# Attention layer of a graph network: column-tiled denominators, products on GpSimd, normalisation on ScalarE, next batch's rows made early

## The chip, the cores and the metric

One core of a Trainium2 chip. The metric is the time of one launch on the device in microseconds; smaller is better. An execution is called fast when it lies within 1.5% of the fastest of its kernel, and all runs quoted here are fast ones. Engines in the profile: PE is TensorE's matmuls, PEld its weight loads, DVE VectorE, ACT ScalarE, POOL GpSimd, SP SyncE, which issues most of the DMA transfers.

## The reference, cut to what matters

Eight batches of 2048 nodes with 256 features go through two layers. Layer 0, the only one that the change touches, is masked attention with four heads of 64:

```
h = relu(layernorm(x))                           # the "hidden rows"
q, k, v = h @ Wq.T + bq, ...                     # 4 heads x 64
s = clip(q k^T / 8, -10, 10);  s = -10 where adj == 0
ctx = softmax(s) @ v                             # per head
out = layernorm(ctx @ Wo.T + bo + h) * gamma + beta
x = x + out
```

Layer 1 is another graph attention over the same adjacency.

## The kernel before

A group is 512 query rows of a batch; a batch has four groups. Per group the kernel walks over the keys in eight steps of 256. A step has, for each pair of heads, two score matmuls with their mask step on VectorE and their exponential on ScalarE, and the weighted sum of the values. The sums of the exponentials (the denominators of the softmax) are gathered for half a group, 16 step-and-pair tiles in two halves of 8, then inverted and multiplied on, half a group late:

```python
def add_keys(b, g, j, p):                        # GpSimd halves TensorE's work
    t = work.tile([P, 2, 512], F32, tag="es", name="es", bufs=2)
    nc.gpsimd.tensor_tensor(t, es[b, g, j, p, 0], es[b, g, j, p, 1], op=ALU.add)

def denominators(b, g, j, p):
    # ...  two 64-column tiles at once, one row of pz per step and pair
    for s in range(2):
        nc.tensor.matmul(pz[0][ds(s * D, D), :], strip[:, 63 - r : 127 - r], t[:, s, :], ...)
    if last:                                     # once per half group
        nc.scalar.copy(zs, pz[0])                # sums to DRAM, back spread over 128 partitions
        # ... zd <- zs, zi <- zd
        nc.vector.reciprocal(zi, zi)
        # ... zr <- zi

def scale(b, g, j, p):                           # one tile of 128 x 512
    rz = work.tile([P, 512], F32, tag="rz", name="rz", bufs=4)
    for s in range(2):                           # each of two rows to 64 partitions
        nc.sync.dma_start(rz[ds(s * D, D), :], src[s : s + 1, :].to_broadcast([D, 512]))
    # ... the product:
    nc.vector.tensor_tensor(t, t, rz, op=ALU.mult)
    nc.gpsimd.tensor_tensor(dst, dst, t, op=ALU.add)      # the accumulation

def finish(b, g):
    # ... output projection po from acc; hidden row, bias and residual on VectorE into y
    layernorm_stats(work, y, ymv, yrs)           # ends with the power (var + eps)^-0.5 on GpSimd
    for i in range(4):
        normalize(y[:, i, :], y[:, i, :], ymv[:, i, 0:1], yrs[:, i : i + 1])   # VectorE
    nc.gpsimd.tensor_tensor(y, y, rg, op=ALU.mult)
    # ... + beta, + x, then a store to x1d from GpSimd's queue
```

The whole program is recorded first. A scheduler then lays down the order of each engine's queue, and each engine works through its own in that order, waiting where an operand or buffer isn't ready.

The softmax here doesn't subtract the row's maximum and nothing guards it: scores larger than these inputs give would overflow.

Of the kernel before, what the change touches and what calls it, by code (L numbers as in the profile page):

```python
# [25 lines left out]
def kernel(  # L26
# [74 lines left out]
    with ExitStack() as c0:  # L101
# [10 lines left out]
        R = NP * CHALF  # L112
        zd = dram.tile([B, NG, 2, 2, R, 512], F32, tag="zd", name="zd")
        zr = dram.tile([B, NG, 2, 2, R, 512], F32, tag="zr", name="zr")

# [16 lines left out]
        strip = wp.tile([P, 127], F32, tag="strip", name="strip")  # L132
        nc.vector.memset(strip, 0.0)
        nc.vector.memset(strip[:, 63:64], 1.0)
# [8 lines left out]
        for j2 in range(NB // 2):  # L143
            tag = ("hT", "kT")[j2 % 2]
            a_sb = big.tile([P, 2, N], I32, tag=tag, name=f"a_sb_{j2}")
            nc.sync.dma_start(a_sb, adj_t[ts(j2, 2 * P), :].rearrange("(j p) i -> p j i", p=P))
            for k in range(2):
                j = 2 * j2 + k
                e01 = work.tile([P, N], BF16, tag="e", name=f"e01_{j}", bufs=5)
                nc.vector.tensor_scalar(e01, a_sb[:, k, :], 0.0, None, op0=ALU.not_equal)  # L150
                nc.scalar.activation(m0t[:, j, :], e01, AF.Copy, bias=-LIM, scale=2.0 * LIM)
                g01 = work.tile([P, N], BF16, tag="e", name=f"g01_{j}", bufs=5)
                nc.vector.tensor_scalar(g01, a_sb[:, k, :], 0.0, None, op0=ALU.is_gt)
                m1b = work.tile([P, N], I8, tag="ut", name=f"m1b_{j}", bufs=18)
                nc.scalar.copy(m1b, g01)
                nc.gpsimd.dma_start(m1d[:, j, :], m1b)
                for i in range(NIG):
                    for c in range(2):
                        nc.tensor.matmul(
                            degs[i][:, c, :], ones_b, g01[:, ts(2 * i + c, 512)],  # L160
                            start=(j == 0), stop=(j == NB - 1),
                        )
        nn = work.tile([P, N], BF16, tag="es", name="nn", bufs=2)
# [31 lines left out]
        hT, kT, v, mv, rs = {}, {}, {}, {}, {}  # L195

        def prepare0(b):
            hT[b] = big.tile([P, FC, N], F32, tag="hT", name=f"hT_{b}")
            kT[b] = big.tile([P, FC, N], F32, tag="kT", name=f"kT_{b}")
            v[b] = big.tile([P, NB, H, D], F32, tag="v", name=f"v_{b}")  # L200
            mv[b] = work.tile([P, NB, 2], F32, tag="mv", name=f"mv_{b}")
            rs[b] = work.tile([P, NB], F32, tag="rs", name=f"rs_{b}")
            for g in range(NG):
                xg = load_x(b, g, "x")
                layernorm_stats(work, xg, mv[b][:, ts(g, 4), :], rs[b][:, ts(g, 4)])
                pts = ps_sc.tile([P, FC, 512], F32, tag="sc", name="pts")
                for i in range(4):
                    ib = 4 * g + i
                    z = work.tile([P, F], F32, tag="z", name="z", bufs=3)
                    normalize(z, xg[:, i, :], mv[b][:, ib, 0:1], rs[b][:, ib : ib + 1])  # L210
                    for c in range(FC):
                        nc.tensor.transpose(pts[:, c, ts(i, P)], z[:, ts(c, P)], ident)
                for c in range(FC):
                    nc.scalar.activation(hT[b][:, c, ts(g, 512)], pts[:, c, :], AF.Relu)
                hg = hT[b][:, :, ts(g, 512)]
                project_t("k", hg, kT[b][:, :, ts(g, 512)])
                pv = ps_sc.tile([P, 4, F], F32, tag="sc", name="pv")
                for i in range(4):
                    for c in range(FC):
                        nc.tensor.matmul(  # L220
                            pv[:, i, :], hg[:, c, ts(i, P)], wts["v"][:, c, :],
                            start=(c == 0), stop=(c == FC - 1),
                        )
                for i in range(4):
                    nc.vector.tensor_tensor(
                        v[b][:, 4 * g + i, :, :].rearrange("p h d -> p (h d)"),
                        pv[:, i, :], reps["v"], op=ALU.add,
                    )

            project_q(b, 0)  # L230
# [7 lines left out]
        def scores(b, g, j, p, k):  # L238
# [7 lines left out]
            e = work.tile([P, 2, 512], F32, tag="e", name="e", bufs=5)  # L246
# [3 lines left out]
            es[b, g, j, p, k] = e  # L250

        sums, pu, ut, pz = {}, {}, {}, {}

        def add_keys(b, g, j, p):

            t = work.tile([P, 2, 512], F32, tag="es", name="es", bufs=2)
            nc.gpsimd.tensor_tensor(t, es[b, g, j, p, 0], es[b, g, j, p, 1], op=ALU.add)  # L257
            sums[b, g, j, p] = t

        def weighted(b, g, j, p, k):  # L260
            if k == 0:
                pu[0] = ps_u.tile([P, 512], F32, tag="u", name="pu")
            e = es.pop((b, g, j, p, k))
            for s in range(2):
                nc.tensor.matmul(  # L265
                    pu[0][ds(s * D, D), :], v[b][:, 2 * j + k, 2 * p + s, :], e[:, s, :],
                    start=(k == 0), stop=(k == 1),
                )
            if k == 1:
                t = work.tile([P, 512], F32, tag="ut", name="ut", bufs=18)  # L270
                nc.scalar.copy(t, pu[0])  # L271
                ut[b, g, j, p] = t

        def denominators(b, g, j, p):

            r = p * CHALF + j % CHALF
            if j % CHALF == 0 and p == 0:
                pz[0] = ps_z.tile([P, 512], F32, tag="z", name="pz")
            t = sums.pop((b, g, j, p))
            last = j % CHALF == CHALF - 1 and p == NP - 1  # L280
            for s in range(2):
                nc.tensor.matmul(  # L282
                    pz[0][ds(s * D, D), :], strip[:, 63 - r : 127 - r], t[:, s, :],
                    start=(j % CHALF == 0 and p == 0), stop=last,
                )
            if last:
# [3 lines left out]
                for s in range(2):  # L290
                    nc.sync.dma_start(zd[b, g, w, s], zs[ds(s * D, R), :])
                n = 2 * R * 512 // P
                zi = work.tile([P, n], F32, tag="zi", name="zi", bufs=2)
                flat = "s r i -> (s r i)"
# [5 lines left out]
        def scale(b, g, j, p):  # L300

            src = zr[b, g, j // CHALF, :, p * CHALF + j % CHALF, :]
            rz = work.tile([P, 512], F32, tag="rz", name="rz", bufs=4)
            for s in range(2):
                nc.sync.dma_start(rz[ds(s * D, D), :], src[s : s + 1, :].to_broadcast([D, 512]))
# [4 lines left out]
            if j == 0:  # L310
                nc.vector.tensor_tensor(dst, t, rz, op=ALU.mult)
            else:
                nc.vector.tensor_tensor(t, t, rz, op=ALU.mult)  # L313
                nc.gpsimd.tensor_tensor(dst, dst, t, op=ALU.add)  # L314

        def finish(b, g):
            xg = load_x(b, g, "xr")
            y = work.tile([P, 4, F], F32, tag="y", name="y", bufs=1)
            for i in range(4):
                ib = 4 * g + i  # L320
                po = ps_m.tile([P, F], F32, tag="m", name="po")
                for p in range(NP):
                    nc.tensor.matmul(  # L323
                        po, acc[b, g][:, p, ts(i, P)], wts["o"][:, p, :],
                        start=(p == 0), stop=(p == NP - 1),
                    )
                z = work.tile([P, F], F32, tag="z", name="zr", bufs=3)
                normalize(z, xg[:, i, :], mv[b][:, ib, 0:1], rs[b][:, ib : ib + 1])
                nc.vector.tensor_tensor(y[:, i, :], po, reps["o"], op=ALU.add)
                nc.vector.scalar_tensor_tensor(  # L330
                    y[:, i, :], z, 0.0, y[:, i, :], op0=ALU.max, op1=ALU.add
                )
            ymv = work.tile([P, 4, 2], F32, tag="ymv", name="ymv")
            yrs = work.tile([P, 4], F32, tag="yrs", name="yrs")
            layernorm_stats(work, y, ymv, yrs)
            for i in range(4):
                normalize(y[:, i, :], y[:, i, :], ymv[:, i, 0:1], yrs[:, i : i + 1])
            rg = reps["g"].unsqueeze(1).to_broadcast([P, 4, F])
            re = reps["e"].unsqueeze(1).to_broadcast([P, 4, F])
            nc.gpsimd.tensor_tensor(y, y, rg, op=ALU.mult)  # L340
            nc.gpsimd.tensor_tensor(y, y, re, op=ALU.add)
# [3 lines left out]

        later = {}

        order = [prepare0, scores, add_keys, weighted, denominators, scale, project_q, finish]
# [3 lines left out]

        n = 0
        for b in range(B):
            at(n, prepare0, b)
            for g in range(NG):
                if g + 1 < NG:
                    at(n + 24, project_q, b, g + 1)
                for j in range(NJ):
                    for p in range(NP):  # L360
                        for k in range(2):
                            at(n, scores, b, g, j, p, k)
                            at(n + 2, weighted, b, g, j, p, k)
                            n += 1
                        at(n - 1, add_keys, b, g, j, p)
                        at(n + 4, denominators, b, g, j, p)
                    if j % CHALF == CHALF - 1:
                        for i in range(R):
                            at(n + 11 + i, scale, b, g, j - CHALF + 1 + i // NP, i % NP)
                at(n + 24, finish, b, g)  # L370
# [248 lines left out]
```

## Time and profile before

| | before |
|---|---|
| time | 5824.49 us, median of 3 runs (5818.94 to 5836.31) |
| end of the last output projection of layer 0 | 3690 us |
| TensorE's waiting in layer 0 (below) | 454 us |
| granted TensorE clock | 0.963 of full speed |

"TensorE's waiting" is my own count from the trace: for every two matmuls that follow each other, the distance of their starts less the usual distance of such a pair (0.43 to 0.53 us), summed where it is over 0.1 us. It includes matmuls that run slow for a while after a stop.

First, what the reciprocals' tiles (rz) do. This is the tile's view: operation, engine, count, then least, median and largest duration in ns; below, what ended the idle time ahead of the operations on this tile.

```profile
L305 SPq DMA_DIRECT2D rz<-zr x1024: 444/594/1547, 177.5 to 3672.7; - x171
...
  DMA rz<-zr: 89.6, 90
```

1024 loads (two a tile), and in the whole run engines stood idle 89.6 us for them. The second view lists waits by pairs: engine and line that waited, what it waited for, total in us, times, longest.

```profile
PE sc L242 <- DVE e L248: 181.2, 96, 6.0
...
DVE e L248 <- POOL es L257: 103.4, 36, 3.6
...
DVE y L93 <- POOL yrs L90: 51.1, 32, 2.7
```

TensorE's chief wait is for the mask step, because VectorE frees the scores' PSUM buffers; VectorE's wait for the power (yrs) is 1.6 us a group.

### The profile page before, as it was taken

The page shows a single profiled execution, that of the slowest core. Times are in us where ns is not written, and L with a number is a line of the kernel's source. Part 1 is how long each engine was busy: PE and PEld are TensorE (multiplying, and loading weights), DVE is VectorE, ACT ScalarE, POOL GpSimd, SP SyncE. Part 2 cuts the span into 40 slices and gives each one's busy share as a digit, 9 for nine tenths or more (in the row PEclk, how much of TensorE's full clock was granted, in tenths as well). Part 3 has the DMA queues.
Part 4 walks back from the last instruction along what each step waited for, and adds up shares of the span by engine and source line. Part 5 has one row for each costly group of instructions (what it writes and reads, how often), then busy time and mean ns, then how long its engine had stood idle before and what let it go on. Part 6 is the DMA issues. An engine that isn't in the chain of part 4 may idle for free.

```text
span 5821.8 us, 50880 instructions
## 1 busy us (share of the span) xinstructions
PE 5352.1 (92%) x17648; PEld 1757.2 (30%) x17648; DVE 4122.9 (71%) x5366; ACT 1750.8 (30%) x2441; POOL 2648.0 (45%) x1599
## 2 busy tenths in 40 slices
PE   6998998998998998998998999499999999999999
PEld 2223223223223222322322322233333333333333
DVE  4675676676676666567566667588888888888887
ACT  5443443443443443443343344100010010000100
POOL 2665665665665666566566566412120312212121
PEclk8999999999999999999999999799999999999999
DMA  5121111112121111111111121201010110101010
GB/s 184 46 60 52 53 52 61 43 55 68 38 57 58 51 53 52 48 56 58 49 53 58 40 60 53 104 8 51 8 58 0 58 37 22 51 8 58 0 44 15
DMA packets 173651, 288.63 MB, mean 50 GB/s; under 512 B 40240, under 2 KB 91312, under 8 KB 167088
## 3 DMA queue, kind: packets, MB, share of 16 engines
q1 hardware_dynamic: 162640, 247.36, 13.8%
q0 software_dynamic: 10752, 38.02, 1.8%
q8 instruction: 138, 2.26, 0.2%
q14 instruction: 121, 0.99, 0.1%
HBM read 243.08 MB, written 42.21 MB: 49 GB/s over the span
## 4 chain that ended last, share of the span: by engine, by line
PE 65%; DVE 11%; issue 8%; DMA 7%; POOL 7%; SPq 1%; ACT 1%; DVEq 0%; POOLq 0%; ACTq 0%
PE av L503 21%; PE sc L242 15%; PE pu L265 13%; PE pz L282 5%; PE pp L181 3%; DVE w L491 3%; DVE e L248 3%; POOL nnm L477 3%; PE po L323 2%; DMA rz<-zr 2%; PE pv L220 2%; DVE ut L313 2%; PE pq L451 1%; POOL acc L314 1%; DMA x<-x1d 1%
## 5 line engine op out<-in xcount | busy, mean ns | idle before, releaser
L248 DVE SCALAR_TENSOR_TENSOR e<-sc,m0t 128x1024 f32<-128x1024 f32 x1024 | 1243.2, 1220 | 819.2 <-PE sc L242 714.7
L503 PE MATMUL av<-w,q 128*65 128x512 f32 x4096 | 1795.3, 595 | 28.6 <-DVE w L491 28.6
L257 POOL TENSOR_TENSOR es<-e 128x1024 f32<-128x1024 f32 x512 | 1225.5, 2397 | 896.7 <-PE pz L282 804.6
L491 DVE SCALAR_TENSOR_TENSOR w<-rrep,tcol,m1t 128x1024 f32<-128x1024 f32 x1024 | 1352.1, 1346 | 236.3 <-PE av L503 232.2
L242 PE MATMUL sc<-qT,kT 64*128 64x512 f32 x4096 | 1242.9, 655 | 182.7 <-DVE e L248 181.2
L249 ACT ACTIVATE e<-e 128x1024 f32<-128x1024 f32 x1024 | 1083.8, 1058 | 1038.0 <-DVE e L248 1007.5
L265 PE MATMUL pu<-e,v 128*64 128x512 f32 x4096 | 1196.6, 639 | 0.5
L503 PEld LDWEIGHTS av<-w,q 128*65 128x65 f32 x4096 | 559.9, 139 | 1150.7 <-issue 1061.4
L314 POOL TENSOR_TENSOR acc<-acc,ut 128x512 f32<-128x512 f32 x448 | 651.2, 1466 | 378.9 <-DVE ut L313 376.8
L539 POOL TENSOR_TENSOR x<-x,hp 128x256 f32<-128x256 f32 x128 | 148.0, 1170 | 1469.5 <-DVE hp L535 1469.1
L242 PEld LDWEIGHTS sc<-qT,kT 64*128 64x128 f32 x4096 | 330.8, 188 | 1046.8 <-DVE e L248 599.9
L282 PE MATMUL pz<-es,strip 128*64 128x512 f32 x2048 | 564.2, 607 | 3.1 <-POOL es L257 3.1
L313 DVE TENSOR_TENSOR ut<-ut,rz 128x512 f32<-128x512 f32 x448 | 523.8, 1186 | 52.5 <-DMA rz<-zr 51.7
L271 ACT COPY ut<-pu 128x512 f32<-128x512 f32 x512 | 298.2, 582 | 687.8 <-PE pu L265 686.8
L265 PEld LDWEIGHTS pu<-e,v 128*64 128x64 f32 x4096 | 215.0, 137 | 797.6 <-ACT e L249 387.5
L510 ACT COPY u<-av 65x1024 f32<-65x1024 f32 x64 | 64.5, 1008 | 1242.5 <-PE av L503 1242.5
L282 PEld LDWEIGHTS pz<-es,strip 128*64 128x64 f32 x2048 | 153.4, 140 | 307.4 <-issue 282.5
L477 POOL TENSOR_SCALAR nnm<-mean,nnc 128x256 f32<-128x256 f32 x128 | 197.1, 1557 | 7.4 <-ACT mean L474 7.3
L323 PE MATMUL po<-wo,acc 128*128 128x256 f32 x512 | 153.2, 421 | 50.6 <-POOL acc L314 39.3
L93 DVE TENSOR_SCALAR z<-x,mv,rs 128x256 f32<-128x256 f32 x256 | 119.0, 509 | 93.1 <-POOL rs L90 50.7
L89 POOL TENSOR_SCALAR bnve<-mv 128x4 f32<-128x4 f32 x64 | 27.9, 436 | 268.4 <-DVE mv L87 268.4
L86 DVE BATCH_NORM_STATS2 bnst<-x 128x6 f32<-128x256 f32 x256 | 97.8, 405 | 72.0 <-DMA x<-x1d 47.0
(82 smaller groups left out, 2959.8 us busy)
## 6 DMA issues: line engine op xcount, KB each, us to landing
rz<-zr SPq DMA_DIRECT2D x1024, 128.0 KB
rrep<-rd SPq DMA_DIRECT2D x32, 1024.0 KB
a_sb<-in_adj_t_dram SPq DMA_DIRECT2D x8, 2048.0 KB
x<-in_x_dram SPq DMA_DIRECT2D x32, 512.0 KB
xr<-in_x_dram SPq DMA_DIRECT2D x32, 512.0 KB
x1d<-y POOLq DMA_DIRECT2D x32, 512.0 KB, 5.2
x<-x1d SPq DMA_DIRECT2D x32, 512.0 KB
out_dram<-x POOLq DMA_DIRECT2D x32, 512.0 KB, 3.5
```

The costliest lines, as they stand in the source:

```text
L242: nc.tensor.matmul(sc[:, s, :], kT[b][hs, p, ts(2 * j + k, P)], qT[b, g][hs, p, :], start=True, stop=True,)
L248: nc.vector.scalar_tensor_tensor(e, sc, -LIM, m, op0=ALU.max, op1=ALU.min)
L249: nc.scalar.activation(e, e, AF.Exp, scale=SCALE)
L257: nc.gpsimd.tensor_tensor(t, es[b, g, j, p, 0], es[b, g, j, p, 1], op=ALU.add)
L265: nc.tensor.matmul(pu[0][ds(s * D, D), :], v[b][:, 2 * j + k, 2 * p + s, :], e[:, s, :], start=(k == 0), stop=(k == 1),)
L271: nc.scalar.copy(t, pu[0])
L282: nc.tensor.matmul(pz[0][ds(s * D, D), :], strip[:, 63 - r : 127 - r], t[:, s, :], start=(j % CHALF == 0 and p == 0), stop=last,)
L313: nc.vector.tensor_tensor(t, t, rz, op=ALU.mult)
L314: nc.gpsimd.tensor_tensor(dst, dst, t, op=ALU.add)
L477: nc.gpsimd.tensor_scalar(nnm[b][:, i, :], mean, nnc[:, i : i + 1], None, op0=ALU.mult)
L491: nc.vector.scalar_tensor_tensor(w, rrep[b, h][:, ts(ig, 1024)], tcol[b][:, j, h : h + 1], m1t[:, j, ts(ig, 1024)], op0=ALU.max, op1=ALU.mult,
L503: nc.tensor.matmul(pav[0][:, k, :], q1[b][:, j, h, :], w[:, ts(k, 512)], start=(j == 0), stop=(j == NB - 1),)
```

## The change

The intent: take 512 sums off GpSimd by giving the exponentials straight to TensorE in four 32-column tiles; give GpSimd the products instead, so that VectorE is free for the mask steps; normalise on ScalarE; make the next batch's hidden rows during the batch before.

```diff
-        def denominators(b, g, j, p):
+        def denominators(b, g, j, k):
...
-            for s in range(2):
+            for h in range(H):
                 nc.tensor.matmul(
-                    pz[0][ds(s * D, D), :], strip[:, 63 - r : 127 - r], t[:, s, :],
+                    pz[0][ds(32 * h, 32), :], strip[:, 31 - r : 63 - r],
+                    es[b, g, j, k, h // 2][:, h % 2, :],
+                    start=first, stop=last, tile_position=(0, 32 * h),
                 )
...
             rz = work.tile([P, 512], F32, tag="rz", name="rz", bufs=4)
-            for s in range(2):
-                nc.sync.dma_start(rz[ds(s * D, D), :], src[s : s + 1, :].to_broadcast([D, 512]))
+            nc.sync.dma_start(
+                rz,
+                bass.AP(
+                    tensor=src.tensor, offset=src.offset,
+                    ap=[[CHALF * 512, 2], [0, D], [1, 512]],
+                ),
+            )
...
-                nc.vector.tensor_tensor(t, t, rz, op=ALU.mult)
+                nc.gpsimd.tensor_tensor(t, t, rz, op=ALU.mult)
                 nc.gpsimd.tensor_tensor(dst, dst, t, op=ALU.add)
...
         def finish(b, g):
             y = work.tile([P, 4, F], F32, tag="y", name="y", bufs=1)
             for i in range(4):
-                ... hidden row, bias and residual on VectorE after the projection
+                nc.scalar.activation(
+                    y[:, i, :], xg[:, i, :], AF.Relu,
+                    bias=nb[b][:, ib : ib + 1], scale=rs[b][:, ib : ib + 1],
+                )
...
             for i in range(4):
-                normalize(y[:, i, :], y[:, i, :], ymv[:, i, 0:1], yrs[:, i : i + 1])
+                nc.scalar.activation(y[:, i, :], y[:, i, :], AF.Identity, bias=..., scale=...)
...
-            at(n, prepare0, b)
+            for g in range(NG):
+                at(n - S + 4 + 7 * g if b else -1, hidden, b, g)
+                at(n + 8 * g - (2 if g else 0), project_k, b, g)
+                at(n + 8 * g, project_v, b, g)
...
-                at(n + 24, finish, b, g)
+                at(n + 22, finish, b, g)
```

The cuts leave out that e has six buffers for five, that the products are recorded two steps earlier (n + 9 for n + 11), and that the bias bo is added on GpSimd.

## The prediction

> **What bounds the kernel now.** I read the page from the top, then the groups, then the chain of waits inside one batch of layer 0 (1600 to 1700 us), then the timeline of the same stretch. Layer 0 runs to about 3690 us, layer 1 after it is not touched.
>
> ```profile
> PE 5352.1 (92%) x17648; PEld 1757.2 (30%) x17648; DVE 4122.9 (71%) x5366; ACT 1750.8 (30%) x2441; POOL 2648.0 (45%) x1599
> PE   6998998998998998998998999499999999999999
> ```
>
> TensorE is the bound in both layers; the recurring 8 in layer 0 says that it also waits. In the steady stretch it does not: one pair of heads and 256 keys is two scores, two weighted sums and one denominator, 1.06 + 1.01 + 1.06 + 1.01 + 0.86 = 4.99 us without a gap.
>
> ```profile
> 1604.27 1.06 PE sc L242 x4
> 1605.32 1.01 PE pu L265 x4
> 1606.33 1.06 PE sc L242 x4
> 1607.39 1.01 PE pu L265 x4
> 1608.40 0.86 PE pz L282 x4
> ```
>
> A batch has 64 of these. The starts of the query projections in the timeline are about 66, 98.4, 99 and 184 us apart, 446 us for a batch, while 64 x 4.99 is 319. Projections, transposes and the output product add some 70, matmuls of a pair that the scheduler split (they run alone, at twice the price) some 10. I counted the excess of each gap between matmul starts over its usual value: about 47 us a batch, 375 in all, is waiting. It comes in two places per group of 512 rows.
>
> ```profile
> 1623.15 1.01 PE pu L265 x4
> ...
> 1625.46 2.12 issue
> 1627.58 1.72 POOL acc L314
> ...
> 1629.62 1.05 POOL yrs L90
> ...
> 1633.02 1.14 DVE e L248
> ...
> 1634.21 1.37 PE sc L242 x4
> 1635.58 1.90 PE pu L265 x4
> ```
>
> First, in the finish of the group before: the little power on GpSimd (yrs) stands behind sums and accumulations in that queue; VectorE waits for it ahead of the next mask step, and TensorE runs dry for 4 us, then goes slow for a few matmuls (1.90 for 1.01). Second, 50 us later, the products with the reciprocals crowd VectorE: another 5 us.
>
> ```profile
> 1672.08 3.25 DMA rz<-zr
> ...
> 1680.53 1.22 DVE e L248
> ...
> 1681.79 2.08 PE sc L242 x4
> ```
>
> So a group loses about 11 us, and the start of each batch some 18 more. The two operations that change places, with mean time and what they waited for:
>
> ```profile
> L314 POOL TENSOR_TENSOR acc<-acc,ut 128x512 f32<-128x512 f32 x448 | 651.2, 1466 | 378.9 <-DVE ut L313 376.8
> L313 DVE TENSOR_TENSOR ut<-ut,rz 128x512 f32<-128x512 f32 x448 | 523.8, 1186 | 52.5 <-DMA rz<-zr 51.7
> ```
>
> **What the Trainium skill says.** TensorEngine Tiling (Array Packing), Available Configurations and Key Properties: 128x32 gives four independent tiles, and changing the tiling mode drains TensorE. The trace agrees on the drain: last pass of a weighted sum to a score takes 0.53 us, to a denominator of the same 64-column mode 0.43. TensorE: Matmul & The Clock Gate, Part 1 on queue depths: VectorE and ScalarE are strict FIFO, which is what the 1629 to 1634 wait shows. GPSIMD Engine Reference, opening: elementwise work is about twice as slow there as on VectorE. Agreed: 128x512 with two inputs takes 0.65 us on VectorE at its least (L313), 1.25 on GpSimd (L314); the VectorE mean of 1.19 is time lost to sharing. ScalarE: Activation LUTs, What ACT_TABLE_LOAD costs: 186 ns, 93 for each pointer operand, 0.833 a column, so about 0.58 us for a 256-wide normalisation, 0.5 back to back; here the nearest is the 512-wide projection at 0.68 with one pointer.
>
> **The change part by part.**
> 1. Denominators. 512 sums of 2.36 us leave GpSimd (1225 us). TensorE now feeds four heads' weights straight in, eight passes instead of four for each 128 keys, every second step as before. If four 32-column tiles run together as two 64-column tiles do now (their passes start 7 ns apart), the call stays two passes of 0.43. But the weighted sum ahead of it is in 64-column mode: one more switch, 0.10 of drain plus some 0.03 of weight load seen (the 64-column load shows 0.05). 512 x 0.13 = 67 us more on TensorE.
> 2. Products to GpSimd: 512 x 1.28 = 655 us there, 620 us off VectorE. GpSimd's sum stays below half of layer 0, so it is no throughput bound. The second wait of 5.5 us a group goes: nothing that VectorE or ScalarE does in that stretch waits for products.
> 3. Normalisation to ScalarE, 384 of 0.5 us, about 200 us over 3500; it was a third busy. Harmless in sum, but its place in the queue matters.
> 4. Next batch's rows early: the 18 us a batch at the boundary is spread; I leave 6 of it.
> 5. The finish moves two steps earlier (22 for 24), and this is where I expect the gain to be given back. In the built program's order, GpSimd has 11 products and accumulations of the next group's first half ahead of the power (groups 0 and 1; 12 or 14 in others). They cannot begin before the reciprocals are back. Count from T0, the last denominator of that half: the reciprocal stands behind the third mask step after T0 (T0+7.6; now it runs at T0+4.7), then 0.55, the store 1.5, issue 0.5, the load about 3.1: first product at T0+13 (measured now: T0+10.5). Then 11 x 1.31 + 1.3 = 15.7, so the power is done at T0+28.8. VectorE's scaled mean waits for it, ScalarE's four normalisations (2.1) after that, and behind them in ScalarE's queue the query projection's eviction (1.3), which the seventh score needs for its PSUM buffer: T0+32.3. What TensorE has before that: six scores with one split pair 7.4, six weighted sums 6.1, three denominators 3.0, output product 3.5, projection 3.6: 23.6. So it stands for 8.7 us and then pays about 1.8 at the slow clock: 10.5, as much as both waits of today.
> 6. The other groups by the same count: the third, with hidden rows' statistics also waiting on GpSimd, 14; the fourth, whose transposes wait for ScalarE, 15; the first of a batch, with key and value projections to fill in, 10. With the 6 of part 4: 56 us of waiting a batch against 47.
>
> Sum: per batch +9 waiting, +8.4 switches, -2 for fewer split pairs, hence about +15, with 8 batches +120. A second count by intervals (101 for 98.8, 105 for 98.6, 249 for 249) gives +9 a batch, +72. Start and tail of layer 0 about +3: the last half's products cost GpSimd 2.6 us a tile, but the output product comes as late now. I take the lower half of that: 5824 + 76 = 5900.
>
> **The rivals.**
> (a) The waits vanish, as intended. TensorE would keep 67 us of switches and 50 of waits: 5824 - 375 + 67 + 50 = about 5570. For it: VectorE loses nearly half its work in layer 0, and both waits run through VectorE. Against: the power, not VectorE's own work, ended the first wait, and its queue on GpSimd has grown.
> (b) Four tiles do not run together but two and two: 512 x 0.86 = 440 us more work, part of it into the waits, some 6150. Against: two streams overlap perfectly here, and the page lists the four-tile form. No trace of the kernel before shows four.
> (c) GpSimd as a steady bound: 30 operations x 1.31 + four wide ones x 2.4 + 3 = 52 us of a 100 us group; no.
> (d) The reciprocal's round trip is shorter than I count, by 3 us: finish waits 7 to 8 us, then 5800.
>
> **Range and chances.** The step that decides is the wait in the finish, 32 times: 3 us of error is 100 us. Range 5730 to 6030, centre 5900. Over 2% is below 5708 or above 5941: faster 0.12, same 0.50, slower 0.38; the slower side has (b) and the larger of my two sums.
>
> **What would show it.** Right: the denominators' group at about 0.99 us a call with eight passes, four starting within some 20 ns; in the chain, once a group, GpSimd products and accumulations, then yrs, VectorE's small step, ScalarE's y, the query eviction and only then a score, with 8 to 10 us of TensorE idle; no wait in the other half; 100 us and more between query projections. Wrong: idle before the scores under 3 us a group (rival a), denominators at 1.7 us a call (rival b), or a first product before T0+10.

## The result, and the profile after

The changed kernel is correct and much slower.

| | before | after |
|---|---|---|
| time, median | 5828.82 us (4 runs) | 7060.53 us (4 runs) |
| range of the runs | 5818.94 to 5836.31 | 7055.6 to 7065.65 |
| end of the last output projection of layer 0 | 3690 us | 4925 us |
| TensorE's waiting in layer 0 | 454 us | 1610 us |
| granted clock, profiled run | 0.963 | 0.883 |

The ratio of the fast runs is 1.211, 95% interval 1.209 to 1.214. Ratios here are the mean time of one kernel's fast runs over that of the other's in the same rounds, so not quite the ratio of the medians. All 1235 us are lost in layer 0. The page's head after:

```profile
PE 5495.1 (78%) x19696; PEld 1726.8 (24%) x19696; DVE 3252.6 (46%) x4246; ACT 1926.9 (27%) x2825; POOL 2053.6 (29%) x1631
...
PE   6777766777766677776677757773899999999999
...
PEclk8888887888887898887888878886999999999999
```

TensorE is busy 143 us more in the sum, but in layer 0 its share has fallen to some 70%: it stands still most of the time that was added. No engine has a larger share of its time busy than before; so it is a wait, not a load. VectorE and GpSimd are both far emptier, as the change meant them to be.

The tile's view of rz says where to look:

```profile
L313 SPq DMA_DIRECT2D rz<-zr x512: 479/4888/8209, 176.2 to 4893.9; - x171
...
  DMA rz<-zr: 2731.5, 503
```

Half as many loads, but SyncE's queue is held 4.9 us by the median one where it was 0.6, and engines stand idle 2731.5 us until such loads land, thirty times as long as before. Not all of this is the load's doing: GpSimd has less work now and often rests until the first product of a half. Ahead of the other seven products of each half it idles 1390 us, where VectorE idled 19 in the kernel before (my own sums from the traces). The list of waits shows how that travels:

```profile
POOL ut L327 <- DMA rz<-zr: 2176.6, 442, 45.5
ACT y L354 <- DVE ynb L200: 1179.1, 32, 65.6
DVE ynb L200 <- POOL yrs L90: 1120.1, 32, 41.6
...
PE sc L255 <- ACT qT L185: 527.7, 17, 37.9
PE pu L272 <- ACT e L262: 425.4, 37, 42.2
PE pv L236 <- ACT qT L185: 250.4, 8, 35.8
```

The second and the third have a count of 32: once a group, some 35 us each. TensorE's three sum to 1203 us. One such block in the timeline (start in us, duration, engine, operation; in brackets the idle time ahead of it and what ended it):

```profile
1645.06 1.26 POOL L327 TENSOR_TENSOR ut<-ut,rz 128x512 f32<-128x512 f32 x1 [3.95 <-DMA rz<-zr]
...
1650.27 1.26 POOL L327 TENSOR_TENSOR ut<-ut,rz 128x512 f32<-128x512 f32 x1 [2.61 <-DMA rz<-zr]
...
1671.06 1.26 POOL L327 TENSOR_TENSOR ut<-ut,rz 128x512 f32<-128x512 f32 x1 [3.73 <-DMA rz<-zr]
1672.28 1.04 POOL L90 TENSOR_TENSOR yrs<-bnve,mhalf 128x4 f32<-128x4 f32 x1
...
1673.36 1.23 DVE L200 SCALAR_TENSOR_TENSOR ynb<-mv,yrs 128x4 f32<-128x4 f32 x1 [37.44 <-POOL yrs L90]
1674.62 2.07 ACT L354 ACTIVATE y<-y,ynb,yrs 128x256 f32<-128x256 f32 x4 [38.81 <-DVE ynb L200]
...
1676.60 1.24 ACT L185 ACTIVATE qT<-pp,bq 128x512 f32<-128x512 f32 x2
...
1677.89 2.08 PE L255 MATMUL sc<-qT,kT 64*128 64x512 f32 x4 [37.39 <-ACT qT L185]
```

Read it from the top: products come 5.2 us apart although one takes 1.26, each waiting for its load; the power stands behind eight of them; VectorE's small step waits 37.4 us for the power, ScalarE's normalisations for that, the query eviction stands behind those, and the score needs the PSUM buffer that the eviction frees. The last four matmuls take 2.08 us for the usual 1.06: after the stop the granted clock is 0.50 of full speed (1677.8 to 1680 us), where it is 1.00 from 1604 to 1609 us. This is the chain of my step 5, link by link, four times as long.

The trace also has every DMA packet. Counted over the stream of layer 0, packets of 2048 bytes (a row of rz for one partition; median 84 ns in both kernels) were in flight 8.66 at a time on average before, and 2.08 at a time after, exactly two in 89% of the time. So a tile of 128 such packets takes 128 x 84 / 2 ns = 5.4 us. The Trainium skill has this, on a page that I had not opened for the prediction: DMA: Bandwidth & Descriptors, section Why a DMA increments its semaphore by 16 and not by 1, says that the number of DMA engines is the largest one up to 16 that divides the slowest dimension of both patterns, and that the lowest-numbered engines are taken. Outermost dimension 2, two engines; this trace agrees (which two they are it does not tell).

### The profile page after: what moved, and what is told of

It reads as the page before. It is cut to its first block, busy times and chain, and to the rows that moved or that the text cites. A ratio compares the mean times of both kernels' runs of the same rounds, so it can differ in the third digit from the quotient of the medians.

```text
span 7053.8 us, 53409 instructions
## 1 busy us (share of the span) xinstructions
PE 5495.1 (78%) x19696; PEld 1726.8 (24%) x19696; DVE 3252.6 (46%) x4246; ACT 1926.9 (27%) x2825; POOL 2053.6 (29%) x1631
## 3 DMA queue, kind: packets, MB, share of 16 engines
q8 instruction: 155, 2.54, 0.2%
## 5 line engine op out<-in xcount | busy, mean ns | idle before, releaser
L255 PE MATMUL sc<-qT,kT 64*128 64x512 f32 x4096 | 1268.2, 664 | 570.1 <-ACT qT L185 527.7
L272 PE MATMUL pu<-e,v 128*64 128x512 f32 x4096 | 1172.1, 638 | 425.7 <-ACT e L262 425.4
L327 POOL TENSOR_TENSOR ut<-ut,rz 128x512 f32<-128x512 f32 x448 | 569.1, 1270 | 2185.7 <-DMA rz<-zr 2176.6
L288 PE MATMUL pz<-e,strip 128*32 128x512 f32 x4096 | 580.4, 622 | 0.0
L328 POOL TENSOR_TENSOR acc<-acc,ut 128x512 f32<-128x512 f32 x448 | 561.2, 1268 | 10.0
L354 ACT ACTIVATE y<-y,ynb,yrs 128x256 f32<-128x256 f32 x128 | 66.4, 589 | 1179.1 <-DVE ynb L200 1179.1
L236 PE MATMUL pv<-wv,hT 128*128 128x256 f32 x512 | 134.2, 421 | 250.4 <-ACT qT L185 250.4
L345 PE MATMUL po<-wo,acc 128*128 128x256 f32 x512 | 187.0, 516 | 153.3 <-POOL acc L328 148.5
L325 POOL TENSOR_TENSOR acc<-ut,rz 128x512 f32<-128x512 f32 x64 | 81.2, 1269 | 574.3 <-DMA rz<-zr 555.0
L288 PEld LDWEIGHTS pz<-e,strip 128*32 128x32 f32 x4096 | 83.5, 109 | 446.0 <-issue 406.3
```

The lines of the kernel that those rows point to most:

```text
L255: nc.tensor.matmul(sc[:, s, :], kT[b][hs, p, ts(2 * j + k, P)], qT[b, g][hs, p, :], start=True, stop=True,)
L272: nc.tensor.matmul(pu[p][ds(s * D, D), :], v[b][:, 2 * j + k, 2 * p + s, :], e[:, s, :], start=(k == 0), stop=(k == 1),)
L288: nc.tensor.matmul(pz[0][ds(32 * h, 32), :], strip[:, 31 - r : 63 - r], es[b, g, j, k, h // 2][:, h % 2, :], start=first, stop=last, tile_ ...
L327: nc.gpsimd.tensor_tensor(t, t, rz, op=ALU.mult)
L345: nc.tensor.matmul(po[:, i, :], acc[b, g][:, p, ts(2 * i2 + i, P)], wts["o"][:, p, :], start=(p == 0), stop=(p == NP - 1),)
```

## The experiments

Every kernel gave the correct result. Each stands beside runs of the kernel before from the same rounds; ratios are to those.

**Theories.** A: the single load paces the products, and these hold up what stands behind them in GpSimd's queue. B: products on GpSimd, or the new order of the finish, cost the time by themselves. C: the four-tile denominators do. D and E came up on the way and are told in section 2; F, named in one expectation, is many small waits of VectorE and ScalarE together.

### 1. The load, undone and added; the denominators alone; the products moved back

The changed kernel with two loads:

```diff
-            nc.sync.dma_start(rz, bass.AP(..., ap=[[CHALF * 512, 2], [0, D], [1, 512]]))
+            for s in range(2):
+                nc.sync.dma_start(
+                    rz[ds(s * D, D), :], src[s : s + 1, :].to_broadcast([D, 512])
+                )
```

> The changed kernel with one thing undone: each tile of reciprocals (rz, 128x512) is again loaded by two DMAs of 64 partitions instead of one DMA over both rows. Theory A (the single load has only two packets of 84 ns in flight and takes 5.2 us a tile, it paces the products, and these hold the power in GpSimd's queue): products 1.3 us apart, the idle time that ends with a load of rz falls from 2731 us to under 300 us, the time falls from 7060 to 5800-5950 us. Theory B (products on GpSimd and the order of the finish cost the time by themselves): over 6700 us, with the same 8 to 10 us or more of idle TensorE behind each power. Theory C (four-tile denominators): over 6700 us.

Measured: 5919.49 us, ratio 1.015 (1.013 to 1.017). 1141 of the lost us are back, as theory A said, and B and C fall as the main cause. Two signs that I had put down for A missed. The products come 2.6 us apart and not 1.3, because accumulations stand between them, and the idle time is far over 300 us:

```profile
  DMA rz<-zr: 1713.0, 97
```

It is the sign that was badly chosen: in 97 waits for 503, nearly all of it is GpSimd resting ahead of the first product of a half; ahead of the other seven it idles 21 us for the 1390 above.

The kernel before with the single load (the reverse edit):

> The kernel before with one thing added: each tile of reciprocals is loaded by one DMA over both rows (outermost dimension 2) instead of two DMAs. Theory A: a tile takes about 5.2 us, and the products, here in VectorE's queue between the evictions of the scores, pace these: 8 tiles x (5.2 - 2.5) us x 64 halves = 1380 us at most, so 6500-7300 us. Theory B or C (the load is incidental): within 2% of 5825 us.

Measured: 7704.82 us, ratio 1.321. Slower than the upper end I gave, and far from "incidental": the load alone, in a kernel with none of the other changes, costs 1870 us. There the products sit in VectorE's queue and hold the scores' mask steps directly:

```profile
DVE ut L318 <- DMA rz<-zr: 1845.9, 427, 8.4
```

The kernel before with the denominators of the change and nothing else (no `add_keys`, four 32-column tiles, heads inside keys, six buffers of e):

> The kernel before with the denominators of the change alone: four 32-column tiles over 128x512, no sums on GpSimd, keys outer and heads inner; products stay on VectorE, loads stay two. Theory A with my step 1: 512 calls x 0.13 us = +67 us, less what the wait for GpSimd's sums cost: 5800-5930 us. Theory C (four tiles cost the time): over 6400 us.

Measured: 5656.38 us, ratio 0.970 (0.968 to 0.971). Faster than I allowed for (5800 at the least). The groups of the denominators' matmuls, before and then here (count, busy us, mean ns):

```profile
L282 PE MATMUL pz<-es,strip 128*64 128x512 f32 x2048 | 564.2, 607 | 3.1 <-POOL es L257 3.1
```

```profile
L274 PE MATMUL pz<-e,strip 128*32 128x512 f32 x4096 | 567.4, 605 | 0.0
```

Twice the matmuls in the same busy time, and the starts of four lie 6 or 7 ns apart: four tiles do run together. (Matmuls that start together like this are a pass.) The call costs what I had worked out: the distances from the last weighted sum to the first pass, between the passes, and to the next score are 0.529, 0.453 and 0.543 us, where they were 0.429, 0.429 and 0.529, so 0.138 more a call, 71 us in 512. What I had too small is the gain on the other side: TensorE's waiting falls from 503 to 263 us (counted up to 4000 us). In the kernel before, VectorE's mask steps waited 103.4 us for GpSimd's sums, which held the buffers of e, and TensorE 181.2 us for the mask steps; here the first wait doesn't exist and the second is this:

```profile
PE sc L241 <- DVE e L247: 78.3, 51, 6.7
```

Theory C is refuted in sign. What part of the gain is due to the missing sums, to the sixth buffer or to the new order of heads and keys, this one run does not tell.

The changed kernel with the products back on VectorE, single load kept:

> The changed kernel with the products back on VectorE and the single load kept. Theory A: still slow, 6500-7300 us, now with VectorE's products waiting for loads of rz and the scores' evictions behind them. Theory B (GpSimd as the place of the products): 5800-6000 us.

Measured: 7669.17 us, ratio 1.315. GpSimd is not the cause; with the slow load VectorE is an even worse place for the products. It came out above the range I gave for A, as the single load in the kernel before did; by what the excess comes I have not followed up.

### 2. What is left with two loads: 87 us over the kernel before, 263 over the four tiles alone

The waits of the kernel with two loads show a new one:

```profile
ACT y L332 <- DMA x1d<-y: 281.5, 31, 12.2
PE pu L272 <- ACT e L262: 210.7, 31, 9.8
...
DVE ynb L200 <- POOL yrs L90: 99.8, 32, 5.2
```

L332 is ScalarE's first write to y in the finish, `Relu` of the input rows, which depends on nothing but an early load. In the built program the scheduler has put it 5 to 11 instructions behind the last normalisation of the group before, and 50 to 65 ahead of its own. But y has one buffer, and the group before is still in GpSimd's three wide operations and its store. So ScalarE waits about 9 us, once a group, with the exponentials behind it, and TensorE 6.8 us for those. Three tries: two buffers for y (theory D: this wait), products on VectorE (theory E: the power behind the products, my step 5), and both.

```diff
-            y = work.tile([P, 4, F], F32, tag="y", name="y", bufs=1)
+            y = work.tile([P, 4, F], F32, tag="y", name="y", bufs=2)
```

> The changed kernel with the two loads of 64 partitions, and with two buffers for y instead of one. With the loads mended 5919 us remain, 87 over the kernel before. Theory D (ScalarE's first write to the next y stands 10 instructions after the last normalisation of the one before, waits there for the store to x1d, 281.5 us in 31 waits, and holds up an exponential for which TensorE then waits 210.7 us): that wait goes, and 5919 falls by 150 to 240 us, to 5680-5770 us. Theory E (my step 5: the power behind the products of the next group in GpSimd's queue): the wait for y is incidental, 5860-5930 us.

> The changed kernel with the two loads and the products back on VectorE, y left with one buffer. Theory D: the wait of ScalarE for the store of y stays, 5850-5950 us. Theory E (step 5: GpSimd's queue with the products ahead of the power costs the time): 5680-5780 us, the wait of VectorE for the power (99.8 us in 32 waits) gone.

> The changed kernel with the two loads, two buffers for y, and the products back on VectorE: both suspects taken away. Theory D: as with two buffers of y alone, within 40 us of it. Theory E: as with the products on VectorE alone. If both count, faster than either; below 5656 us (the kernel before with the four tiles alone) if the early rows then pay their 12 us a batch, 8 batches, 96 us: 5560-5640 us.

Measured: 5910.22 us (two buffers), 5895.91 (products on VectorE), 5885.49 (both). The first two results speak against each other: two buffers alone lie in the range that I had given for E, products on VectorE alone in that for D. Both together bring no more than 34 us. The trace says why for the first:

```profile
ACT y L332 <- DMA x1d<-y: 272.9, 30, 12.1
```

The wait is still there. With a second buffer the scheduler moved the write one more group ahead, right behind the release of *that* buffer. So the run did not test theory D at all. To test it, the write has to be kept late. Its bias is now copied through an operation that reads the reciprocals of the group's second half:

```diff
                 nc.vector.reciprocal(zi, zi)
+                if w == 1:
+                    nbg[b, g] = work.tile([P, 4], F32, tag="nbg", name=f"nbg_{b}_{g}")
+                    nc.vector.scalar_tensor_tensor(
+                        nbg[b, g], zi[:, 0:4], 0.0, nb[b][:, ts(g, 4)],
+                        op0=ALU.mult, op1=ALU.add,
+                    )
...
-                    bias=nb[b][:, ib : ib + 1], scale=rs[b][:, ib : ib + 1],
+                    bias=nbg[b, g][:, i : i + 1], scale=rs[b][:, ib : ib + 1],
```

> The changed kernel with the two loads, y left with one buffer, and ScalarE's first write to y made to depend on the reciprocals of its own second half (its bias is copied through an operation that reads them), so that it can no longer stand in ScalarE's queue right behind the last normalisation of the group before. With two buffers alone that write had only moved one group further ahead and the wait stayed (272.9 us), so that run did not test it. Theory D (ScalarE waiting for the store of y holds up the exponentials): the wait for the store falls from 281.5 us to under 30, TensorE's wait for exponentials from 210.7 to under 80, and 5919 us falls to 5700-5790. Theory E (power behind the products) or F (many small waits of VectorE and ScalarE): 5880-5930 us.

Measured: 5627.79 us, ratio 0.966 (0.965 to 0.967). Theory D stands, with more than I had given it (5700 to 5790): 292 us, more than the wait itself, and this kernel is **3.4% faster than the one before**, the fastest of all, 28 us ahead of the four tiles alone (by the ratios, 0.966 for 0.970, some 22). The products ahead of the power are the same in number as before this edit (the table in section 4), so a new order there is not what helped. The same write, by its group's line (count, busy us, mean ns, then idle time ahead of it):

```profile
L338 ACT ACTIVATE y<-xr,nbg,rs 128x256 f32<-128x256 f32 x128 | 67.6, 590 | 5.6 <-DVE nbg L309 5.1 <-issue 0.2
```

281.5 us of idle time ahead of it have become 5.6. In TensorE's list of waits that of the weighted sums for the exponentials is no longer there.

> The same with the products on VectorE. Theory D alone: within 25 us of the late write alone. Theory E adds: another 60 us or more less. If VectorE's load costs something: more than the late write alone. I expect 5670-5770 us.

Measured: 5711.62 us, ratio 0.980. With the two defects mended, moving the products back to VectorE costs 84 us; so GpSimd is the right place for them. That the same move gained 24 us while the early write was there says little of the move itself: ScalarE's wait for the store of y shrank with it, from 281.5 to 172.2 us.

The early rows by themselves, on the kernel before with the four tiles (all normalisation and products still on VectorE):

> The kernel before with the four tiles and, in addition, the rows of the next batch made early as in the change (hidden rows during the batch before, keys and values in four steps); all normalisation stays on VectorE, products on VectorE, two loads. My step 4 (18 us of a batch's waits become 6, 8 batches): 96 us less than 5656, so 5540-5600 us. If the early rows only move the waits into the stream of the batch before: 5630-5690 us.

Measured: 5759.75 us, ratio 0.988: 103 us slower than the four tiles alone (5656). Neither of my two outcomes. TensorE now waits 90.5 us for VectorE's normalised rows in the middle of the stream (`pts`), where before it waited for them at the boundary. The fastest kernel has the early rows with the normalisation on ScalarE beside them; whether they pay there, and what each of the two would give alone, no run shows.

### 3. How the slow load reaches TensorE

> The changed kernel with the single load kept and only ScalarE's first write to y made late. Theory A (the load sets the pace, the early write is hidden behind the same wait): 6850-7060 us. If the two costs simply add (292 us): 6730-6800 us. If the early write was needed for the large loss: under 6300 us.

Measured: 6858.71 us, ratio 1.177. With the single load, the late write brings 202 of its 292 us; most of the loss stays, as A said, just above the lower end of its range.

Next the power of the finish on ScalarE in place of GpSimd, single load kept, early write kept. This is not free: in each group ScalarE then loads a table ahead of the logarithm and another ahead of the exponential, 64 loads of 1283 ns, 82 us in this run.

```diff
-            scaled_stats(y, yrs, ynb)                    # power on GpSimd
+            # ... same statistics on VectorE
+            nc.scalar.activation(yrs, ymv[:, :, 1], AF.Ln, bias=epst[:, 0:1])
+            nc.scalar.activation(yrs, yrs, AF.Exp, scale=-0.5)
+            # ... ynb as before
```

> The changed kernel with the single load kept; in the finish the power of the variance is taken on ScalarE (logarithm, then exponential of minus one half) instead of GpSimd, so no product stands ahead of it. Theory A by way of my step 5 (the power waits behind products that come 5.2 us apart): VectorE's 1120 us of waiting for the power go, and 7060 falls to 5850-6250 us. If late products as such hold TensorE (late output projection, full buffers): it stays over 6700 us. Tables of ScalarE may have to be loaded twice or four times a group: up to 32 x 5 us = 160 us of ScalarE, part of it seen.

Measured: 6984.06 us, ratio 1.198: only 76 us better. That spoke for late products as such. But the list of waits shows other guests in the same queue:

```profile
ACT y L337 <- DMA x1d<-y: 687.1, 31, 40.8
DVE nb L202 <- POOL rs L92: 540.0, 32, 38.1
```

The wait for the power is gone, and at once ScalarE waits up to 40.8 us for the store of y and VectorE up to 38.1 for the *other* power, that of the next batch's hidden rows. Both pass through GpSimd's queue behind the same products. So all three were taken out together: both powers on ScalarE, and the late first write.

> The changed kernel with the single load kept, both powers of layer 0 (finish and hidden rows) on ScalarE, and the late first write to y: nothing that another engine needs soon stands behind the products in GpSimd's queue, and the products come as late as before (5.2 us apart). Theory A1 (the loss is whatever stands behind the products in that queue): the 36 us blocks of TensorE go, 5750-6200 us; what stays is some 5 us a group for the output projection waiting for the last accumulation. Theory A2 (late products as such: output projection, buffers of weighted sums, DMA queue): over 6600 us.

Measured: 6052.81 us, ratio 1.038 (1.036 to 1.039), in the range of A1. The loads are as slow as ever in it:

```profile
L326 SPq DMA_DIRECT2D rz<-zr x512: 479/4922/8474, 181.4 to 3889.0; - x171
...
  DMA rz<-zr: 1861.8, 490
```

and GpSimd still idles 1862 us for them (1899 with the late write alone), but that idling costs TensorE far less now. That settles A1: against the single load with the late write alone (6858.71) 806 us are gone, though no product comes sooner (the last product of a half ends 48.0 us after the start of its reciprocal, 47.6 there; medians). They were not lost by late products, but by what other engines need from behind them in GpSimd's queue. What remains, 425 us over the fastest kernel, is in part the output projection waiting for the last accumulation:

```profile
PE po L358 <- POOL acc L341: 177.9, 26, 62.7
```

ScalarE also has 98 table loads, 126 us, for the two powers; the rest I have not taken apart.

The counterpart, with quick loads:

> The kernel with two loads and the late first write to y (5628 us), with the power on ScalarE as well. My step 5 (10.5 us a group behind the power, 32 groups, 336 us): 5300-5450 us. What its trace shows (VectorE waits 94.5 us for the power in 32 waits, TensorE hardly at all): within 40 us of 5628, or above it by the loading of tables.

Measured: 5634.78 us, ratio 0.966, the same as with the power on GpSimd (5627.79). The move has a price of its own:

```profile
L362 ACT ACT_TABLE_LOAD x32 | 41.1, 1283 | 0.6
L363 ACT ACT_TABLE_LOAD x32 | 41.1, 1283 | 0.6
```

These 82 us of ScalarE come in, and VectorE still waits 78.3 us for the power, now from ScalarE. So with quick loads this way of taking the power from behind the products gains nothing; that the wait there (VectorE 94.5 us) costs nothing is not shown by it.

### 4. The load's speed apart from the order of the queue

One thing confuses the first experiment: the two loads changed the *order* as well. In the built program of the changed kernel 11, 12, 14 and 14 products and accumulations (7 or 8 products) of the next half stand ahead of the power in the four groups of a batch; with two loads only 4, 5, 6 and 9 (3 to 6 products). The scheduler reckons the loads differently and lays the queue out anew. A source pattern with zero steps changes the speed and leaves the order:

```diff
-                    rz[ds(s * D, D), :], src[s : s + 1, :].to_broadcast([D, 512])
+                    rz[ds(s * D, D), :],
+                    bass.AP(tensor=row.tensor, offset=row.offset,
+                            ap=[[0, c], [0, D // c], [1, 512]]),      # c = 4, or 2
```

The first try was on the kernel with two loads and nothing else, c = 4:

> The changed kernel with two loads of 64 partitions each, the source written as 4 x 16 x 512 with zero steps instead of 64 x 512. If the number of DMA engines follows the slowest dimension of the pattern (theory A), each load keeps 4 packets of 84 ns in flight and takes 16 x 84 ns = 1.3 us; two loads of a tile on the same engines 2.7 us, on different ones 1.3 us: up to 8 packets in flight, and 5910-6150 us. If the pattern is merged to 64 x 512 again, or the number of engines comes from the length alone: as with two plain loads, 5919 us within 10, with the packets as parallel as there.

Measured: 6087.64 us, ratio 1.044, against 5919 with the plain two loads. Packets in flight: 3.86 on average, four in 73% of the time, where the plain loads have 8.57. So the pattern is not merged, the number of engines follows its outermost dimension, and both loads of a tile share the same four engines: SyncE's queue is held only 0.5 us by a load here, so that two loads overlap in time, and on different engines eight packets would be in flight. Then the fastest kernel with c = 2 and c = 4:

> The best kernel so far (two loads, late first write to y, 5628 us) with each load's source written as 2 x 32 x 512 with zero steps: the order of the queue stays that with 4 to 9 operations ahead of the power, the load becomes as slow as the single one (two packets in flight, 128 x 84 / 2 ns = 5.4 us a tile). With the single load and the late write, 7.75 products a group stood ahead and 1231 us were lost. If the loss is products ahead of the power times the pace of the load: 4.25 products a group, so about half of it, 6100-6450 us. If the speed alone counts and the order does not: 6800-6900 us. If the order alone counts: under 5700 us.

> The same with the source written as 4 x 16 x 512: four packets in flight, 2.7 us a tile, hardly slower than a product and an accumulation on GpSimd (2.54 us). The loss should nearly vanish: 5640-5800 us. A loss in proportion to the load's time (2.7 of 5.4 us, half of what two engines lose) would be over 5850 us.

Measured: 6325.10 us with two engines (2.06 packets in flight, ratio 1.085), 5838.19 with four (3.86 in flight, ratio 1.001). VectorE's wait for the power, in the fastest kernel, with four engines and with two:

```profile
DVE ynb L200 <- POOL yrs L90: 94.5, 32, 5.5
```

```profile
DVE ynb L200 <- POOL yrs L90: 262.9, 32, 12.1
```

```profile
DVE ynb L200 <- POOL yrs L90: 573.2, 32, 25.0
```

With the order held, the speed alone costs 697 us; the single load with the long queue (6858.71, same late write) costs 1231. So with the slow load somewhat more than half of the loss is the load's pace over the 3 to 6 products that stand ahead in any case, and the rest its pace over the further ones that the single load's order put there.

Two engines came out where I expected. Four engines missed, 210 us where I had 12 to 172: I compared 2.7 us a tile with a product *and* an accumulation (2.54), but ahead of the power stand mostly products, at 1.27. Worked out again: 4.25 products at the load's pace of 2.75 us are 11.7 us a group against 6 operations at 1.3, 7.8 us, and the first load lands 1.5 us later (median from reciprocal to first product 7.35 us, for 5.88): 5.4 us a group, 172 in 32 groups. VectorE's wait grew by 168.

Last, the nearest I could come to the case that my step 5 had reckoned: quick loads with a long queue. The finish two steps later brings it about, though with two mask steps more for the power to be ready in:

```diff
-                at(n + 22, finish, b, g)
+                at(n + 24, finish, b, g)      # 14, 14, 12, 14 operations ahead of the power
```

> The best kernel (two loads, late first write to y, 5628 us) with the finish two steps later (24 for 22, as in the kernel before): in the built program 14, 14, 12 and 14 operations then stand ahead of the power instead of 4, 5, 6 and 9, with the quick load; VectorE's step that waits for the power also stands two mask steps (5 us) later. My step 5 gives 7.5 operations more x 1.3 = 9.8 us a group, less the 5 us: VectorE's waits for the power go from 94.5 us to about 94.5 + 32 x 4.8 = 250 us, and the time to 5740-5830 us. If a quick load makes the order harmless: within 40 us of 5628.

Measured: 5685.40 us, ratio 0.974. Between the two outcomes: 57 us more than at 22, and VectorE's wait for the power 164.1 us for the 250 expected. The later finish moves other things too, so 57 us, 1.8 a group, is what the long queue and its company cost together.

All of it in one table (medians; products ahead of the power in the four groups of a batch, packets of rz in flight):

| kernel | us | products ahead | in flight |
|---|---|---|---|
| before | 5824 to 5834 | (other order) | 8.7 |
| before, four tiles alone | 5656 | (other order) | 9.2 |
| changed | 7061 | 7, 8, 8, 8 | 2.1 |
| + two loads | 5919 | 3, 4, 4, 6 | 8.6 |
| + two loads, late write | **5628** | 3, 4, 4, 6 | 8.1 |
| same, four engines | 5838 | 3, 4, 4, 6 | 3.9 |
| same, two engines | 6325 | 3, 4, 4, 6 | 2.1 |
| one load, late write | 6859 | 7, 8, 8, 8 | 2.1 |
| one load, late write, no power on GpSimd | 6053 | no power in that queue | 2.1 |

## Why the prediction was wrong, by its own steps

The predicted 5900 us lies 1160 us under the 7060 measured, and outside its range.

1. *Denominators, +67 us.* Right in the cost: 0.138 us a call for 0.13, the four tiles together (rival b, "four tiles do not run together", falls). What I missed stands beside it: alone this part makes the kernel 176 us faster (5656 for the 5832 of the same rounds), and the mask steps' wait for GpSimd's sums, 103.4 us, is gone.
2. *Products to GpSimd, no throughput bound, the second wait goes.* Right: GpSimd is 29% busy, rival c falls, and with everything else in order the products are 84 us better on GpSimd than on VectorE.
3. *Normalisation on ScalarE, "Harmless in sum, but its place in the queue matters."* The size, an estimate from the skill's figures, is right (0.59 us each where it had 0.58, four in 2.07; 204 us in all for "about 200"). The warning is right too, but I did not follow it up for the first write to y: 292 us once the loads are quick, hidden partly behind the larger loss until then.
4. *Early rows, 18 us a batch becoming 6.* Not shown alone as I meant it. With VectorE's normalisation they cost 103 us; beside ScalarE's they are part of the fastest kernel.
5. *The finish.* Here the prediction failed, and in one term: "the load about 3.1". I took the time of a load from the kernel before, where it was two DMAs of 64 partitions, and did not ask what the changed pattern does to it. First product at T0+13 is right for the two loads (7.45 to the reciprocal and 5.9 on, T0+13.3), and came at T0+16.7 with the one. Worse, "11 x 1.31" assumed that the products run at GpSimd's pace. They ran at the load's, 5.2 us: eight products up to the power take 42 us at that pace, where I had 14.4 for eleven operations. The links named (power, VectorE's step, ScalarE's y, query eviction, seventh score) are the ones that the trace shows; the wait was 37.4 us in the block above for the 8.7 reckoned. With quick loads the reckoning was too high instead: the long queue with the finish two steps later cost 57 us, where the same count gave 112 to 202, and VectorE's wait grew by 70 us for some 155.
6. *The other groups, 14, 15 and 10.* Same term, same failure: all 32 groups have a block of some 35 us.

That the expected 5900 lies near the 5919 of the kernel with two loads is a coincidence of sums: there the wait for y's buffer, which I had not foreseen, stands in the place of the wait for the power, which I had. Rival a (5570, the waits vanish as intended) is nearest to what the change is worth once mended, 5628. As to what would show the prediction wrong, I had named idle time that is too short, never too long. Three slips of reading changed nothing: the 512 sums take 2.39 us each, not 2.36; of the two operations that "change places" only the product (L313) moves; and VectorE lost 36% of its work in layer 0 (2411 to 1541 us), not nearly half.

## What to carry to other kernels

Whoever rewrites two transfers as one may have changed their speed: compare the patterns' outermost dimensions before trusting the old duration (the Trainium skill, DMA: Bandwidth & Descriptors, Rules for kernel authors, has the rule as "Use all 16 engines"). An engine that is mostly idle can still hold everything up, when quick little operations that others need stand in its queue behind slow deliveries; count what stands ahead of them, and at whose pace it goes. And check after an experiment that the wait it was to remove is gone: two buffers for y removed nothing, and one removed wait let in two others of the same queue.

## What the Trainium skill lacked or had wrong

- DMA: Bandwidth & Descriptors was right where it mattered here, and I had not read it for this change. With outermost dimension 2, 4 and 64 the runs show 2.1, 3.9 and 8.6 packets in flight on average (the last is no count of engines: it is above eight in half of the time), and with 4 the two loads of a tile shared one set of four engines. Beyond a bandwidth per engine it gives no duration for packets like these; here a 2048-byte packet took 84 ns, and a 128x512 tile on two engines 5.2 to 5.4 us.
- TensorEngine Tiling (Array Packing) says that a change of tiling mode drains TensorE but not what that costs: here 0.10 us when 32-column tiles follow 64-column ones, and 0.138 us for the whole denominator call.
- No page warns that the order of an engine's queue depends on how the scheduler reckons a load: one load in place of two put 11 to 14 operations ahead of the power where 4 to 9 had stood, and a second buffer moved a write one group further ahead, with 272.9 us of waiting left of 281.5.
